# Attention, then top-256 attention, on one core: the first units' scores among the projections, the last five units' fills dealt out anew, the second batch's norm passes one by one

## Chip, core and metric

The kernel runs on one core of a Trainium2 chip. The core has a matrix engine (TensorE, PE in the profile), VectorE (DVE), ScalarE (ACT), GpSimd (POOL) and a queue engine (SyncE, SP) that here only starts transfers. Every engine works through its own instruction list in order and waits on semaphores. The metric is the device time of one execution in microseconds, the lower the better; the figure for a kernel is the median of several runs.

## What is computed

Two layers follow each other on x of 8 x 512 x 32 x 32 (8 batches, 512 channels, 1024 positions), in fp32. Cut to what matters:

```python
# layer 0
h = group_norm(x, 32 groups) * gn_w + gn_b
q, k, v = split(qkv_w @ h + qkv_b)                   # 8 heads of 64
a = softmax(q^T k / 8)                               # 1024 x 1024 per head
x = x + proj_w @ (a v) + proj_b
# layer 1
q, kk, v = wq @ x, wk @ x, wv @ x
idx = top_k(sum over channels of x*x, 256)           # per batch
qs, ks, vs = q, kk, v at idx
a = softmax(clip(LN(qs) LN(ks)^T / sqrt(512), -80, 80))
v at idx = a vs
x = x + wo @ v
```

## The kernel before

**Layer 0** (`layer0`, lines 583 to 1101) is cut into 64 units: 8 batches, 4 pairs of heads, 2 halves of 512 query positions. A unit has 8 steps over key blocks of 128 positions. For each block, PE makes the scores of both heads (`scores`, tile `sc`, a PSUM tile of two banks; two such tiles exist), ScalarE copies them to SBUF (`keep`, tile `e`, 14 buffers) and VectorE keeps a running maximum (`highest`). After the eighth block PE turns the maximum (`turn`, tile `pt`), VectorE reduces and negates it (`negate`, `nm`), PE spreads it back (`spread`, `ns`), VectorE adds it to each kept block (`shift`, "sub"), ScalarE takes the exponential, GpSimd sums the eight blocks (`add`, tile `es`) and PE multiplies them with v (`values`, tile `av`). The sum of all keys goes through PE (`total`, `den`), ScalarE (`take`, `ri`) and VectorE (`invert`, `divide`), giving half of a tile `o`.

The order of all this is written out by hand: `SLOT` (lines 46 to 52) lists the steps of one slot; a plus means that the step is for the next unit, a minus for the one before. All engines but SP follow that order (line 1058). In slot t, then, the scores of unit t + 1 and the exponentials and values of unit t are worked on together.

Between them stand up to five **fills**, `fill0` to `fill4`: blocks of PE work that belong to no softmax. Each is a pair of functions, one for PE and one that empties the PSUM bank. `side(t)` (lines 804 to 827) lists them: projections of q and k (`project`), of v (`v_tokens`), the output projection of the batch before (`project_out`, emptied by VectorE into the residual tile `xr` and then stored), four products `bias_out` in batch 0 that carry v's bias through the output projection, and in the last three units work for layer 1. All fills use one PSUM bank, tile `g` (`ps_g`, one buffer), so a fill waits until the one before it is emptied. Two banks hold `ns` (`ps_m`), one holds `av` (`ps_a`).

Ahead of slot -1 (lines 1069 to 1075) ten fills named `first` run one after the other through that one bank: k and q of the first pair, four parts of v, q of the second pair. Slot -1 then holds unit 0's scores alone.

Group norm of batch b: `norm_stats` reads statistics for one of four channel blocks, `mean_take`, `spread_of`, `variance_take` and `norm_factors` make a factor and a shift, and `norm_apply` rewrites one block of x. For b > 0 these stand in the slots of the batch before, by `NORM` (lines 693 to 699); for b = 1 by `NORM1` in the slots -1 and 0.

**The crossing.** For layer 1, batch 0, `turned_values` and `joint` form wo times wv (tile `wvn`, then `w["vo"]`), `token_rows` transposes x, squares it and stores it, `token_values` makes the values. `begin_layer1` and `finish` (lines 1033 to 1056) hold what is left after unit 63: the last row, all values, the importance of batch 0's tokens and `count_first` (how many tokens lie above each one, on VectorE), and eight output projections of batch 7, each with its own `load_residual` into one of two `xr` buffers. `also` (line 1007) gives each such piece a PSUM bank, two of three from the `sc` tiles, and empties a piece after the next one was filled.

**Layer 1** (`layer1`) follows lists of its own, `BATCH` and `END`, with eight PSUM banks. Its first PE work is `row` of batch 1, tile `b_pt`.

SP starts the loads and stores that these steps name, in an order of its own list; a start that waits holds up those behind it. ScalarE starts the stores of rows (`sx`) and values (`sv`) and the small vectors (`vector_of`, line 146).

## Time and profile before

| what | us |
|---|---|
| median of 3 runs (lowest, highest) | 2684.85 (2680.85, 2687.46) |
| the profiled execution, its time | 2687.3 |
| its span, first to last instruction | 2685.6 |
| PE busy, of the span | 2591.3 (96%) |
| DVE, ACT, POOL busy | 1926.2, 1354.5, 1163.2 |
| mean granted TensorE clock | 0.990 |
| PE busy from 0 to 20, of 20 | 3.5 |
| from 20 to 80, of 60 | 46.86 |
| from 160 to 240, of 80 | 72.50 |
| from 2040 to 2140, of 100 | 82.05 |
| from 2180 to 2200, of 20 | 14.73 |

The profile shows one execution. A line of its timelines has the start, the duration, the engine, the line of the kernel, the operation, the tile written and those read, the shape, how many instructions are merged in it, and in brackets how long the engine was idle before and what ended that idle time. PE's weight loads are a row of their own (PEld). In its table of stretches a group is one engine's busy time with the count of instructions.

### The profile page before, as it was taken

The numbers are of one execution on the slowest core, as the hardware profiler recorded it, in microseconds if no ns is written. First come the engines' busy times: TensorE is split into PE (matmuls) and PEld (weight loads), VectorE is DVE, ScalarE is ACT, GpSimd is POOL, SyncE is SP. The second block draws the span as 40 slices with busy tenths as digits, with TensorE's granted clock in tenths as the row PEclk, the third lists the DMA queues.
The fourth block names the chain that finished last, engine by engine and source line by source line (L and its number), as shares of the span: only waits on it lengthen the run. The fifth ranks groups of instructions, "written<-read, shape, count | busy, mean of one in ns | idle before, by whom it ended". The sixth has DMA issues, their size and how long they took to land.

```text
span 2685.6 us, 27430 instructions
## 1 busy us (share of the span) xinstructions
PE 2591.3 (96%) x9936; PEld 1194.8 (44%) x9936; DVE 1926.2 (72%) x2437; ACT 1354.5 (50%) x1697; POOL 1163.2 (43%) x559
## 2 busy tenths in 40 slices
PE   6999999999999999999999999999998899999995
PEld 3444444444444444444444444444443345555553
DVE  1787878787878688867887787777767636666664
ACT  1555654565556546645665465456555523333331
POOL 0455544455456445445564465445444401211122
PEclk9999999999999999999999999999999999999998
DMA  3000000100100010001000100010002243555555
GB/s 133 1 1 32 1 16 32 48 1 16 62 18 1 24 58 14 1 32 63 0 1 32 63 1 8 24 63 1 16 32 79 75 165 114 197 207 198 194 186 195
DMA packets 79590, 161.21 MB, mean 60 GB/s; under 512 B 12106, under 2 KB 12106, under 8 KB 79456
## 3 DMA queue, kind: packets, MB, share of 16 engines
q1 hardware_dynamic: 52480, 113.27, 11.9%
q10 hardware_dynamic: 19296, 33.58, 3.3%
q0 software_dynamic: 7680, 12.61, 1.6%
q8 instruction: 79, 1.29, 0.2%
q14 instruction: 55, 0.45, 0.1%
HBM read 100.68 MB, written 71.30 MB: 64 GB/s over the span
## 4 chain that ended last, share of the span: by engine, by line
PE 89%; DMA 4%; DVE 3%; ACT 2%; issue 1%; POOL 1%; ACTq 0%; SPq 0%; POOLq 0%; DVEq 0%
PE sc L901 18%; PE av L960 16%; PE g L725 16%; PE g L746 8%; PE g L764 8%; PE b_pv L299 6%; PE b_pp L382 4%; PE den L973 2%; PE ns L938 2%; PE pt L924 2%; DMA sx<-xT 1%; PE last L299 1%; PE b_sc L448 1%; DVE e L944 1%; PE first L725 1%
## 5 line engine op out<-in xcount | busy, mean ns | idle before, releaser
L952 POOL TENSOR_TENSOR es<-es,e 128x1024 f32<-128x1024 f32 x384 | 913.0, 2378 | 327.5 <-ACT e L947 306.7
L909 ACT COPY e<-sc 128x1024 f32<-128x1024 f32 x512 | 508.6, 1013 | 591.5 <-PE sc L901 316.4
L944 DVE TENSOR_TENSOR e<-e,ns 128x1024 f32<-128x1024 f32 x512 | 603.7, 1205 | 2.5 <-PE ns L938 2.2
L947 ACT ACTIVATE e<-e 128x1024 f32<-128x1024 f32 x512 | 531.7, 1056 | 109.5 <-DVE e L944 101.7
L901 PE MATMUL sc<-q,k 64*128 64x512 f32 x2048 | 514.1, 620 | 20.1 <-ACT e L909 17.2
L915 DVE TENSOR_TENSOR high<-sc,high 128x1024 f32<-128x1024 f32 x384 | 469.4, 1222 | 89.2 <-PE sc L901 46.5
L960 PE MATMUL av<-e,v 128*64 128x512 f32 x2048 | 493.6, 603 | 2.7 <-ACT e L947 2.7
L952 POOL TENSOR_TENSOR es<-e,e 128x1024 f32<-128x1024 f32 x64 | 151.4, 2366 | 740.1 <-ACT e L947 740.1
L725 PE MATMUL g<-x,wqkv 128*128 128x512 f32 x976 | 447.6, 601 | 0.0
L901 PEld LDWEIGHTS sc<-q,k 64*128 64x128 f32 x2048 | 177.1, 187 | 349.2 <-issue 178.4
L725 PEld LDWEIGHTS g<-x,wqkv 128*128 128x128 f32 x976 | 176.6, 191 | 224.1 <-issue 224.1
L960 PEld LDWEIGHTS av<-e,v 128*64 128x64 f32 x2048 | 130.0, 136 | 298.6 <-issue 288.5
L985 DVE RECIPROCAL ri<-ri 128x512 f32<-128x512 f32 x64 | 214.6, 3352 | 29.2 <-ACT ri L981 28.8
L746 PE MATMUL g<-wqkv,x 128*128 128x256 f32 x960 | 223.2, 386 | 0.0
L746 PEld LDWEIGHTS g<-wqkv,x 128*128 128x128 f32 x960 | 177.4, 190 | 67.2 <-issue 45.5
L764 PE MATMUL g<-o,wp 128*128 128x512 f32 x448 | 207.2, 605 | 0.0
L299 PE MATMUL b_pv<-w,x 128*128 128x512 f32 x448 | 199.0, 592 | 0.0
L929 DVE TENSOR_REDUCE nm<-pt 128x8 f32<-128x1024 f32 x64 | 78.4, 1224 | 149.5 <-PE pt L924 149.5
L771 DVE SCALAR_TENSOR_TENSOR xr<-g,pb,xr 128x512 f32<-128x512 f32 x56 | 41.9, 749 | 173.1 <-PE g L764 173.1
L764 PEld LDWEIGHTS g<-o,wp 128*128 128x128 f32 x448 | 80.5, 189 | 124.3 <-issue 107.2
L981 ACT COPY ri<-den 128x512 f32<-128x512 f32 x64 | 37.5, 586 | 184.8 <-PE den L973 141.7
L299 PEld LDWEIGHTS b_pv<-w,x 128*128 128x128 f32 x448 | 82.5, 190 | 90.5 <-issue 90.2
(157 smaller groups left out, 2037.5 us busy)
## 6 DMA issues: line engine op xcount, KB each, us to landing
x<-in_x_dram SPq DMA_DIRECT2D x32, 512.0 KB
xr<-in_x_dram SPq DMA_DIRECT2D x64, 256.0 KB
x1d<-xr SPq DMA_DIRECT2D x64, 256.0 KB
x<-x1d SPq DMA_DIRECT2D x32, 512.0 KB
sx<-xT ACTq DMA_DIRECT2D x64, 256.0 KB
sv<-V ACTq DMA_DIRECT2D x64, 256.0 KB
y<-x1d SPq DMA_DIRECT2D x64, 256.0 KB
out_dram<-y SPq DMA_DIRECT2D x64, 256.0 KB
```

The costliest lines, as they stand in the source:

```text
L299: nc.tensor.matmul(pv, x1[b][:, k, ts(j, P)], w["vo"][:, k, :], start=(k == 0), stop=(k == CT - 1),)
L725: nc.tensor.matmul(pq, wqkv[:, k, ts(ot, P)], hs[b][:, k, ts(hf, HALF)], start=(k == 0), stop=(k == CT - 1),)
L746: nc.tensor.matmul(pv[:, ts(j, 2 * P)], hs[b][:, k, ts(2 * part + j, P)], wqkv[:, k, 2 * C + hm * 2 * P : 2 * C + (hm + 1) * 2 * P], start ...
L764: nc.tensor.matmul(po, wp[:, k, ts(mt, P)], os[b * NPAIR + k][:, ts(hf, HALF)], start=(k == 0), stop=(k == CT - 1),)
L901: nc.tensor.matmul(sc[:, hh, :], ks[p][r, ts(j, P)], qs[p][r, ts(hf, HALF)], start=True, stop=True,)
L909: nc.scalar.copy(raw[t, j], banks["s", t, j])
L915: nc.vector.tensor_tensor(high[t], banks["s", t, j], raw[t, 0] if j == 1 else high[t], ALU.max)
L944: nc.vector.tensor_tensor(raw[t, j], raw[t, j], high[t], ALU.add)
L947: nc.scalar.activation(raw[t, j], raw[t, j], AF.Exp, scale=QK_SCALE)
L952: nc.gpsimd.tensor_add(sums[t], raw[t, 0] if j == 1 else sums[t], raw[t, j])
L960: nc.tensor.matmul(avs[t][HD * hh : HD * hh + HD, :], vs[p // 2][:, j, (p % 2) * P + HD * hh : (p % 2) * P + HD * hh + HD], e[:, hh, :], s ...
L985: nc.vector.reciprocal(dens[t], dens[t])
```

## The change

It has five pieces.

1. Ahead of slot -1 only three fills are left: k of the first pair (both halves) and q's first half. They and three more alternate between bank `g` and bank `av`. The three more (q's second half, v's first two parts) are placed in slot -1 after the second, fourth and sixth score block (`FIRST_STEPS`), and their emptying after certain `keep` steps. The other two parts of v and the second pair's q become fills of units 0 and 1, which have five fills each; v_tokens(1, 0) goes from unit 0 to unit 1. The three weight parts are loaded in the order k, q, v, and the vectors `lw` and `lb` are loaded in `constants()`, at slot 2.
2. `bias_out` times four becomes `bias_row` in unit 2 (a row, copied by ScalarE to a buffer of `xr`) and `bias_columns` in unit 3 (four transposes and one add on VectorE).
3. For batch 1 the four statistics stand in slot -1, two after the maximum of block 3 and two after that of block 7, and the four `norm_apply` of slot 3 stand after `div`, after `sub` of block 5, after `sub` of block 6 and after the maximum of block 7.
4. Units 60 to 63: unit 60 has six fills, with project(31, 1, 1) put off to unit 61 and three `turned_values` taken in; unit 61 has the last `turned_values` and three `joint`, unit 62 the last `joint`, three `token_values` and a row, unit 63 two `token_values`, two rows beside the fills, and three output projections of batch 7.
5. `also` empties each piece directly after the next fill, and takes bank `g` at listed counts. `begin_layer1` holds five rows and two values, `finish` five output projections, one value and the counts. The residuals of batch 7 are loaded into free `e` buffers (`spare`), but for two in `xr`.

```diff
-            for part in range(3):
+            for part in (1, 0, 2):
                 nc.sync.dma_start(wqkv[:, :, ts(part, C)], wsrc[:, :, ts(part, C)])
...
             NORM1 = {
-                (-1, "max", 7): [(norm_stats, 0), (norm_stats, 1)],
-                (0, "div", 0): [(norm_stats, 2)], (0, "sub", 5): [(norm_stats, 3)],
+                (-1, "max", 3): [(norm_stats, 0), (norm_stats, 1)],
+                (-1, "max", 7): [(norm_stats, 2), (norm_stats, 3)],
+                (3, "div", 0): [(norm_apply, 0)], (3, "sub", 5): [(norm_apply, 1)],
+                (3, "sub", 6): [(norm_apply, 2)], (3, "max", 7): [(norm_apply, 3)],
             }
...
-                        if b == 1 and at <= 0 and name != "neg":
+                        if b == 1 and name != "neg" and at != 2:
                             todo = NORM1.get((at, name, j), [])
...
-            def bias_out(mt):
+            def bias_row():
                 def fill(pt):
                     for k in range(CT):
                         nc.tensor.matmul(
-                            pt[:, :1], wp[:, k, ts(mt, P)],
-                            bqkv[:, 2 * CT + k : 2 * CT + k + 1],
-                            start=(k == 0), stop=(k == CT - 1),
+                            pt, bqkv[:, 2 * CT + k : 2 * CT + k + 1].broadcast_to([P, P]),
+                            wp[:, k, :], start=(k == 0), stop=(k == CT - 1),
                         )
                 def empty(pt):
-                    nc.vector.tensor_add(pb[:, mt : mt + 1], pt[:, :1], bp[:, mt : mt + 1])
+                    resid["row"] = rp.tile([P, C], F32, tag="xr", name="bias_row")
+                    nc.scalar.copy(resid["row"], pt)
+                return fill, empty
+
+            def bias_columns():
+                def fill(pt):
+                    row_ = resid.pop("row")
+                    for mt in range(CT):
+                        nc.tensor.transpose(pt[:, ts(mt, P)], row_[:, ts(mt, P)], ident)
+                def empty(pt):
+                    nc.vector.tensor_add(pb, pt.rearrange("p (m q) -> p m q", q=P)[:, :, 0], bp)
                 return fill, empty
...
+                if t == 0:
+                    todo = [v_tokens(0, 2), v_tokens(0, 3)] + todo + [project(1, 0, 0)]
+                    return todo
+                if t == 1:
+                    todo += [project(1, 0, 1), v_tokens(1, 0)]
...
-                if 1 <= at <= CT:
-                    if b:
-                        todo += [project_out(b - 1, at - 1, h) for h in range(NH)]
-                    else:
-                        todo.append(bias_out(at - 1))
+                if b and 1 <= at <= CT:
+                    todo += [project_out(b - 1, at - 1, h) for h in range(NH)]
+                if 2 <= t <= 3:
+                    todo.append((bias_row, bias_columns)[t - 2]())
+                if t == UNITS - 4:
+                    held.append(todo.pop(1))
+                    todo = [
+                        todo[0], todo[1], turned_values(0), todo[2], turned_values(1),
+                        turned_values(2),
+                    ]
                 if t == UNITS - 3:
-                    todo += [turned_values(mt) for mt in range(CT)] + [joint(0)]
+                    todo += [held.pop(), turned_values(3)] + [joint(c) for c in range(3)]
                 if t == UNITS - 2:
-                    todo += [joint(c) for c in range(1, CT)] + [token_rows(j) for j in range(2)]
+                    todo += [joint(3)] + [token_values(j) for j in range(3)] + [token_rows(0)]
                 if t == UNITS - 1:
-                    todo += [token_rows(j) for j in range(2, 7)]
+                    todo += [token_values(3), token_values(4)]
+                    todo += [project_out(B - 1, mt, 0) for mt in range(3)]
...
             def also(step):
-                if len(last) % 3 == 2:
+                if count_of[0] in (4, 7, 10, 13, 16):
...
                 step[0](pt)
+                flush()
                 last.append((step[1], pt))
-                if len(last) > 1:
-                    last[-2][0](last[-2][1])
+                count_of[0] += 1
+
+            def flush():
+                while last:
+                    end, pt = last.pop()
+                    end(pt)
...
+            outs = [(CT - 1, 0)] + [(mt, 1) for mt in range(CT)]
             def begin_layer1():
-                also(token_rows(7))
-                also(token_values(0))
+                for one in outs[:2]:
+                    load_residual(B - 1, *one)
+                for one in (
+                    token_rows(3), token_rows(4), token_values(5), token_rows(5), token_rows(6),
+                    token_rows(7), token_values(6),
+                ):
+                    also(one)
                 finite(0, 0)
-                also(token_values(1))
                 tiles["imp", 0] = spare("imp_0")
                 also(importance(0))
                 also(importance(1))
-                also(token_values(2))
-                count_first(0)
-                count_first(1)
+                flush()
+                for j in range(2):
+                    count_first(j)
                 total(UNITS - 1, 0)
             def finish():
-                outs = [(mt, hf) for hf in range(NH) for mt in range(CT)]
                 for i, one in enumerate(outs):
-                    load_residual(B - 1, *one)
+                    if i > 1:
+                        load_residual(B - 1, *one, spare(f"xr_last_{3 + i}")[:, :HALF])
                     also(project_out(B - 1, *one))
-                    if i < 5:
-                        also(token_values(3 + i))
-                    if i < 6:
-                        count_first(2 + i)
-                last[-1][0](last[-1][1])
+                    count_first(2 + i)
+                    if i == 0:
+                        also(token_values(7))
+                count_first(7)
+                flush()
...
-                first = [project(0, which, hf) for which in (1, 0) for hf in range(NH)]
-                first += [v_tokens(0, part) for part in range(2 * NH)]
-                first += [project(1, 0, hf) for hf in range(NH)]
-                for i, (begin, end) in enumerate(first):
-                    pt = ps_g.tile([P, HALF], F32, tag="g", name=f"first_{i}")
-                    begin(pt)
-                    end(pt)
+                FIRST_STEPS = {
+                    ("sc", 1): project(0, 0, 1), ("sc", 3): v_tokens(0, 0), ("sc", 5): v_tokens(0, 1),
+                    ("keep", 0): "empty", ("keep", 3): "empty", ("keep", 4): "empty",
+                }
+                pending = []
+                def first(step):
+                    if step == "empty":
+                        end, pt = pending.pop(0)
+                        end(pt)
+                    else:
+                        pool, tag = ((ps_g, "g"), (ps_a, "av"))[len(firsts) % 2]
+                        firsts.append(step)
+                        pt = pool.tile([P, HALF], F32, tag=tag, name=f"first_{len(firsts)}")
+                        step[0](pt)
+                        pending.append((step[1], pt))
+                firsts = []
+                for step in (
+                    project(0, 1, 0), project(0, 0, 0), "empty", project(0, 1, 1), "empty", "empty",
+                ):
+                    first(step)
...
+                    if t == UNITS - 1:
+                        for mt in range(3):
+                            load_residual(B - 1, mt, 0, spare(f"xr_last_{mt}")[:, :HALF])
                     for name, ahead, j in order:
                         if 0 <= t + ahead < UNITS and (name, t) != ("den", UNITS - 1):
                             STEPS[name](t + ahead, j)
+                        if t == -1 and (name, j) in FIRST_STEPS:
+                            first(FIRST_STEPS[name, j])
                         norms(t, name, j)
+                        if t == UNITS - 4 and name == "empty" and j == 4:
+                            fill(t, 5)
+                        if t == UNITS - 4 and (name, j) == ("exp", 6):
+                            empty(t, 5)
+                        if t == UNITS - 1 and (name, j) == ("fill", 1):
+                            also(token_rows(1))
+                            also(token_rows(2))
```

More of the change, by code (lines that the diff above doesn't have):

```diff
@@ L174, in attention_then_topk_attention @@
     a_dram = [dram.tile([TOP, C], F32, tag=f"sa{b}", name=f"sa{b}") for b in range(B)]
-    lw = vector_of(ln_w, CT, "lw")
-    lb = vector_of(ln_b, CT, "lb")
     before = const.tile([P, P], F32, tag="before", name="before")
@@ L183, in constants @@
     def constants():
+        w["ln_w"] = vector_of(ln_w, CT, "lw")
+        w["ln_b"] = vector_of(ln_b, CT, "lb")
         make_lower_triangular(nc, before, val=1.0, diag=False)
@@ L434, in scale @@
                     t[:, c, :], pt[:, a, :], AF.Identity,
-                    bias=lb[:, c : c + 1], scale=lw[:, c : c + 1],
+                    bias=w["ln_b"][:, c : c + 1], scale=w["ln_w"][:, c : c + 1],
                 )
@@ L438, in scale @@
                 nc.vector.tensor_scalar(
-                    t[:, c, :], pt[:, a, :], lw[:, c : c + 1], lb[:, c : c + 1],
+                    t[:, c, :], pt[:, a, :], w["ln_w"][:, c : c + 1], w["ln_b"][:, c : c + 1],
                     ALU.mult, ALU.add,
@@ L776, in project_out, with load_residual @@
                 return fill, empty
-            def load_residual(b, mt, hf):
-                xr = rp.tile([P, HALF], F32, tag="xr", name=f"xr_{b}_{mt}_{hf}")
+            def load_residual(b, mt, hf, xr=None):
+                if xr is None:
+                    xr = rp.tile([P, HALF], F32, tag="xr", name=f"xr_{b}_{mt}_{hf}")
                 nc.sync.dma_start(xr, x[b, ts(mt, P), ts(hf, HALF)])
@@ L815, in side @@
                     todo.append(v_tokens(m + 1, part))
-                if 1 <= at <= CT:
-                    if b:
-                        todo += [project_out(b - 1, at - 1, h) for h in range(NH)]
-                    else:
-                        todo.append(bias_out(at - 1))
+                if b and 1 <= at <= CT:
[8 more added lines that the diff above has]
+                    ]
                 if t == UNITS - 3:
-                    todo += [turned_values(mt) for mt in range(CT)] + [joint(0)]
+                    todo += [held.pop(), turned_values(3)] + [joint(c) for c in range(3)]
                 if t == UNITS - 2:
-                    todo += [joint(c) for c in range(1, CT)] + [token_rows(j) for j in range(2)]
+                    todo += [joint(3)] + [token_values(j) for j in range(3)] + [token_rows(0)]
                 if t == UNITS - 1:
-                    todo += [token_rows(j) for j in range(2, 7)]
+                    todo += [token_values(3), token_values(4)]
+                    todo += [project_out(B - 1, mt, 0) for mt in range(3)]
                 return todo
+            held = []
             def turned_values(mt):
@@ L1003, in layer0 @@
             FIRST, LAST = by_age[0][2], by_age[-1][2]
-            last = []
+            last, count_of = [], [0]
             def also(step):
-                if len(last) % 3 == 2:
-                    pt = ps_g.tile([P, HALF], F32, tag="g", name=f"last_{len(last)}")
+                if count_of[0] in (4, 7, 10, 13, 16):
+                    pt = ps_g.tile([P, HALF], F32, tag="g", name=f"last_{count_of[0]}")
                 else:
-                    pt = ps_s.tile([P, 2, HALF], F32, tag="s", name=f"last_{len(last)}")[:, 0, :]
+                    pt = ps_s.tile([P, 2, HALF], F32, tag="s", name=f"last_{count_of[0]}")[:, 0, :]
                 step[0](pt)
+                flush()
                 last.append((step[1], pt))
-                if len(last) > 1:
-                    last[-2][0](last[-2][1])
+                count_of[0] += 1
[3 more added lines that the diff above has]
+                    end(pt)
             def importance(j):
```

## The prediction

> **What bounds the kernel now.** I read the page's busy times and chain of waits first, then the timeline of the TensorE (PE) queue where its busy share drops, then the other engines' timelines at those places.
>
> Chain of waits of the page (shares of the span):
>
> ```profile
> PE 89%; DMA 4%; DVE 3%; ACT 2%; issue 1%; POOL 1%; ACTq 0%; SPq 0%; POOLq 0%; DVEq 0%
> ```
>
> PE sets the end. Busy time by stretch (span, then busy us of PE, PEld, DVE, ACT, POOL, then granted clock):
>
> ```profile
> 240.00:280.00 40.00, 40.00 (x162) 17.71 (x160) 32.19 (x27) 24.42 (x28) 19.23 (x9) 1.00 0.00 0
> ```
>
> From 240 to 2040 PE never waits: a unit is the sum of its PE instructions. In the timeline, a unit with three fills repeats every 28.6 us (distance of two `pt` blocks), with five every 35.9. A gain must come from stretches where PE waits or runs at half clock. There are three. First, the beginning (start, busy us, then in brackets the wait before it):
>
> ```profile
> 55.14 3.70 PE L725 MATMUL first<-x,wqkv 128*128 128x512 f32 x8 [0.68 <-ACT v L755]
> 59.62 3.70 PE L725 MATMUL first<-x,wqkv 128*128 128x512 f32 x8 [0.78 <-ACT q L733]
> 63.25 1.99 PE L901 MATMUL sc<-q,k 64*128 64x512 f32 x8
> 67.27 2.39 PE L901 MATMUL sc<-q,k 64*128 64x512 f32 x8 [2.03 <-ACT e L909]
> 72.03 2.96 PE L901 MATMUL sc<-q,k 64*128 64x512 f32 x8 [2.37 <-ACT e L909]
> 77.01 3.78 PE L901 MATMUL sc<-q,k 64*128 64x512 f32 x8 [2.02 <-ACT e L909]
> 80.72 4.88 PE L725 MATMUL g<-x,wqkv 128*128 128x512 f32 x8
> ```
>
> Ten fills share one PSUM bank, so each waits for the previous copy; then unit 0's scores run alone and wait for ScalarE and VectorE, with nothing else on PE; the waits bring half clock (3.78 and 4.88 where 1.99 and 3.70 is usual). Second, the second batch's norm in unit 3, on VectorE, GpSimd and PE:
>
> ```profile
> 191.59 8.30 DVE L686 TENSOR_SCALAR x<-x,gsc,gsh 128x1024 f32<-128x1024 f32 x4
> 188.28 10.34 POOL L952 TENSOR_TENSOR es<-es,e 128x1024 f32<-128x1024 f32 x4 [1.72 <-ACT e L947]
> 203.38 3.79 PE L901 MATMUL sc<-q,k 64*128 64x512 f32 x8 [4.45 <-ACT e L909]
> ```
>
> Four passes stand together on VectorE for 8.30 us and everything behind them is late. Third, the end of layer 0, PE then VectorE:
>
> ```profile
> 2119.11 0.66 PE L238 MATMUL g<-ident,x 128*128 128x128 f32 x4 [3.42 <-ACT xT L246]
> 2130.22 1.11 PE L960 MATMUL av<-e,v 128*64 128x512 f32 x4 [2.71 <-ACT e L947]
> 2196.73 2.82 PE L238 MATMUL b_pt<-ident,x 128*128 128x128 f32 x12 [5.27 <-DVE xr L771]
> 2195.92 0.75 DVE L771 SCALAR_TENSOR_TENSOR xr<-last,pb,xr 128x512 f32<-128x512 f32 x1 [7.11 <-DMA xr<-in_x_dram]
> ```
>
> Units 60 to 63 have small transposes (0.6 us) as fills where others have 3.6 us products, so PE waits for the softmax; then the output projections run back to back, and the last residual load is late.
>
> **What the Trainium skill says.** "SBUF — State Buffer", Who interferes with whom: VectorE and GpSimd share a port pair; a tensor_scalar in its two-port mode and a GpSimd instruction exclude each other for a whole instruction. The trace agrees: a norm pass takes 0.80 us at the least, but a median of 2.02 over all 32, one per GpSimd add in unit 3. "TensorE: Matmul & The Clock Gate", What's actually happening: the clock halves after an idle window of about 3.4 us. Here it halved already after three waits of some 2 us each, so I count half clock wherever such waits cluster, and none after a single wait below 2 us (at 2045 the waits of 1.34 and 0.91 brought none).
>
> **Part 1, the beginning.** A fill costs 3.63 us between two others, a pair of scores 1.92, a kept copy 1.01, a maximum 1.23, a bank's copy 0.59 to 0.69. Laid out from the unchanged first matmul at 17.65 (it waits for the norm; the weights' new order changes nothing there, k having landed as second part already): k0, q0, k1 alternate over two banks without a wait to 30.3. First two scores to 32.3, q1 to 35.9, next two to 37.8, v0 to 41.4. By then ScalarE has kept the third score pair (39.1 to 40.1, after its maximum) but VectorE has two norm_stats inserted (2 x 1.48 us, 39.1 to 42.1) ahead of the next maximum, 43.35: a wait of 1.0. Scores to 44.3, v1 to 48.0, scores to 49.95, v2 to 53.6, transposes to 54.6; the other two statistics end at 54.5, just in time; the negated maximum ends 55.9, sc1 56.85, `ns` begins about 57, against 88.86: 32 us earlier. But seven fills are done there instead of eleven; four come later, 4 x 3.63 = 14.5. Net **17.5**, which is the 6.6 us of bank waits, 6.7 of score waits and 4.3 of half clock, all but 1. If the first score also waits for k1's copy, 0.8 less.
>
> The removed loads of lw and lb free 2 x 0.45 us of ScalarE's queue under the wait for x: nothing. In unit 2 they cost the same 0.9, where ScalarE idles 3.0 us before `ri`: nothing, else 0.9.
>
> **Part 2, units 0 to 4.** PE's excess there is 0.28 + 0.89 + 0.89 + 1.27 + 4.45 + 0.89 of waits and (3.79 - 1.99) + (4.84 - 3.70) of half clock: 11.6. The three 0.89 before `sc6` in units 1, 2 and 4 (in unit 3 it is inside the 4.45) arise because bias_out's add holds VectorE until PE has made the bias, with only 2.7 us of PE work after it. Afterwards units 0 and 1 have five fills, unit 2 a full bias_row (its copy is on ScalarE), unit 4 none: these waits go. Unit 2 keeps 1.27 (norm_factors before `nm`). Unit 3 keeps bias_columns with its add: about 1.0, having less PE work than before. The norm passes, each behind a GpSimd add at up to 2.07: after div, 1.6, hidden (the maximum that it delays ended at 190.5, the score behind it went at 193.2); after sub5, under the 4.3 us that VectorE waits for the bias; after sub6 and max7, 2 x 2.07 under fill 0 (3.6) and the transposes: about 1.1 shows at `pt`. New excess 3.4, bounds 1.3 to 8. bias_row plus columns cost 3.63 + 0.53 for four times 0.98: 0.2 more. Net **8.0**.
>
> **Part 3, units 60 on.** Excess before: unit 60 1.48; unit 61 1.34, 0.91, 1.24, 1.63; unit 62 0.2, 0.28; unit 63 1.80, 1.98, half clock 2.6, 3.42, 1.02, 2.71, half clock 1.5; the crossing 5.27 and half clock after it (28 transposes until 2203) 2.8: together 30.2. After the change PE's work is the same; what is exposed:
> - Unit 60: a small transpose before `sc4` leaves 2.8 us less cover, some 1.2; the pair of transposes sharing the bank and then `sc6`, 1.5.
> - Unit 61: fill 1 still small, 1.24. Products cover the rest.
> - Unit 62: four products and one row. The row's copies on ScalarE (1.4, and its store) delay exp2 and exp6, so the sums on GpSimd: 1.2 at `den`.
> - Unit 63: fill 2 (a projection) shares the bank with token_values(4), whose copy stands behind token_rows(1) (0.60 + 0.19 + 0.58 + 0.33) and two exponentials (2.1): free about 12.4 us after `pt`, wanted at 9.4: 3.0.
> - begin_layer1: five rows cost ScalarE 1.7 each; PE waits about 1. Counts 0 and 1 (3.8) stand before the reciprocal (3.35), which still ends as token_values(7) does.
> - finish: five projections instead of eight; VectorE ends two counts (3.8) and its add about 1.9 after PE. A single wait: no half clock.
>
> Sum 11 to 13, against 30.2: **17**. The SP queue: three residual loads go out before the projections, into exp buffers; the last three stand behind stores and x1 of batch 2, the very last issued some 7 us before it is wanted (4.06 us in the trace). Cover gone costs 2 to 4.
>
> Layer 1 keeps its order and PE is busy 100.00 of 100 us from 2200, then 98, so the shift is carried to the end.
>
> **Sum.** 17.5 + 8.0 + 17 = 42.5. The profiled span is 2685.6 (its run 2687.3); the span becomes 2643. The runs' median is 2684.85, so I forecast 2684.85 - 42.5 = about 2643. Differences below 0.3% (8 us) are about what a measurement of this kernel can tell from no change.
>
> **Rivals.**
> - *The end does not pay* (0.15). Another 12 to 17 us of waits: one bank for all of unit 63's projections, and ScalarE with rows, values and exponentials. For it: ScalarE ends waits there already (3.42, 2.71). Against: it is 50% busy or so. Gain 25.5 and up to 5: 2654 to 2659.
> - *VectorE becomes the bound at the beginning* (0.10). It has about 24 us per unit of 29; statistics and passes at 2.8 (the longest in the trace) would overfill unit 3 (24 + 11 against 29.2, 6 us) and cost about as much ahead of unit 0. Parts 1 and 2 then give 14 instead of 25.5: 2654. Against: the passes may fall between GpSimd's adds at 0.80.
> - *More than forecast* (0.06). Half or all of my 16 us of new waits (1.0 + 3.4 + 12) do not occur: 2627 to 2635.
> - *Slower* (0.04). x1 of batch 0 is loaded on SP only when project(31, 1, 1) has released batch 7's x; that now runs at the end of unit 60, no longer as its second fill. token_values(0) needs it as second fill of unit 62. Issue about 2047, 2 MB at the 249 GB/s seen at 2020 is 8.4 us, so 2058; wanted near 2087. PE waits for every us beyond 29 of delay, and the kernel is slower from 71 us of delay on. A delay of 100 gives 2713. Nothing on SP before it is that late in this trace.
> - *No difference* (0.03): a delay of about 71 by the same wait.
>
> **How the numbers follow.** Forecast 0.62, around 2643. Its own range, from the bounds above (part 2 from 3 to 10, part 3 from 10 to 22), is 2635 to 2654. To hold 8 in 10 the range is 2631 to 2660, taking in most of the first two rivals. Faster is 0.62 + 0.15 + 0.10 + 0.06 = 0.93, the same 0.03, slower 0.04.
>
> **What the profile after would show.** Scores of unit 0 between full fills, `ns` of unit 0 near 57 and no half clock from 22 to 100; no 4.45 in unit 3 and norm passes in four places; a wait near 3 us in unit 63 ahead of the first projection by the bank's copy; row transposes of batch 1 beginning 42 us earlier, less than 2.5 us after the last projection, at full clock. Wrong if `ns` is later than 65, if units 60 to 63 hold over 16 us of PE waits, or if layer 1 is longer than before.

## The result and the profile after

The changed kernel takes 2645.02 us, the median of four runs (2641.74 to 2646.70), against 2685.41 (2680.85 to 2687.46) for the kernel before in the same rounds. The ratio is 0.985, with a 95% interval of 0.9833 to 0.9867: 36 to 45 us less, 40.4 by the medians. The profiled execution took 2641.74, its span is 2640.0, against 2687.3 and 2685.6. The two profiled executions thus lie near opposite ends of their kernels' ranges: their spans differ by 45.6, five more than the medians, and the traces of this section are this pair.

PE still sets the end. Chain of waits on the page of the changed kernel:

```profile
PE 90%; DMA 3%; DVE 3%; ACT 1%; issue 1%; POOL 1%; ACTq 0%; SPq 0%; POOLq 0%; DVEq 0%
```

PE's busy time fell from 2591.3 to 2578.1, though the products are the same but for the bias: 13 us of the 45.6 is, for the most part, work done at full clock that ran at half clock before. The other 32 are waits. The stretch that the prediction took as its rule, 240 to 280, is as before: PE busy 40.00 of 40.

**The beginning.** Timeline of PE, changed kernel:

```profile
16.45 13.54 PE L727 MATMUL first<-x,wqkv 128*128 128x512 f32 x24 [3.88 <-DVE x L686]
29.92 1.99 PE L930 MATMUL sc<-q,k 64*128 64x512 f32 x8
31.84 3.70 PE L727 MATMUL first<-x,wqkv 128*128 128x512 f32 x8
...
42.70 1.13 PE L930 MATMUL sc<-q,k 64*128 64x512 f32 x4 [0.53 <-DVE high L944]
...
55.24 1.13 PE L930 MATMUL sc<-q,k 64*128 64x512 f32 x4 [0.26 <-DVE nm L958]
56.30 1.09 PE L967 MATMUL ns<-ident,nm 128*128 128x128 f32 x8
```

Three fills run without a wait, then scores stand between fills at their usual 1.99. `ns` begins 32.6 us earlier than before (88.86). The table of stretches for 22 to 100, which has PE's busy time third and the granted clock third from the end, says the same of the changed kernel:

```profile
22.00:100.00 78.00, 77.09 (x291) 38.47 (x291) 44.95 (x48) 37.94 (x44) 18.91 (x8) 1.00 0.04 15
```

and of the kernel before:

```profile
22.00:100.00 78.00, 64.60 (x210) 32.47 (x210) 22.44 (x25) 24.45 (x29) 5.26 (x3) 0.93 0.08 29
```

**Units 2 and 3.** The 4.45 us wait and its half clock are gone. Three short waits are left on PE:

```profile
159.08 1.99 PE L930 MATMUL sc<-q,k 64*128 64x512 f32 x8 [1.11 <-DVE nm L958]
180.95 1.99 PE L930 MATMUL sc<-q,k 64*128 64x512 f32 x8 [0.89 <-ACT e L938]
187.50 1.07 PE L953 MATMUL pt<-ident,high 128*128 128x128 f32 x8 [0.94 <-DVE high L944]
```

VectorE's timeline has the four passes in four places, 5.70 us in all where they took 8.30 together:

```profile
167.27 1.35 DVE L686 TENSOR_SCALAR x<-x,gsc,gsh 128x1024 f32<-128x1024 f32 x1
174.39 0.81 DVE L686 TENSOR_SCALAR x<-x,gsc,gsh 128x1024 f32<-128x1024 f32 x1
182.17 2.73 DVE L686 TENSOR_SCALAR x<-x,gsc,gsh 128x1024 f32<-128x1024 f32 x1
187.28 0.81 DVE L686 TENSOR_SCALAR x<-x,gsc,gsh 128x1024 f32<-128x1024 f32 x1
```

**Units 60 to 63 and the crossing**, PE, every wait over 0.5 us:

```profile
2003.37 1.99 PE L930 MATMUL sc<-q,k 64*128 64x512 f32 x8 [0.80 <-ACT e L938]
2013.69 0.66 PE L862 MATMUL g<-ident,pair 128*128 128x128 f32 x4 [1.38 <-ACT wvn L869]
2029.31 1.13 PE L930 MATMUL sc<-q,k 64*128 64x512 f32 x4 [1.23 <-DVE high L944]
2089.38 1.08 PE L1002 MATMUL den<-es,ones 128*64 128x512 f32 x4 [1.22 <-POOL es L981]
2100.33 5.40 PE L766 MATMUL g<-o,wp 128*128 128x512 f32 x8 [2.69 <-ACT V L313]
2126.16 3.70 PE L299 MATMUL last<-w,x 128*128 128x512 f32 x8 [0.91 <-ACT xT L246]
2155.17 1.53 PE L238 MATMUL b_pt<-ident,x 128*128 128x128 f32 x12 [1.77 <-DVE xr_last L773]
```

Unit 63's first projection waits 2.69 us for ScalarE to copy token_values(4) out of the shared bank, and then takes 5.40 instead of 3.70: half clock. Batch 1's transposes start 41.6 us earlier (2196.73 before) and at full clock.

Where the gain lies, by start times of the same instruction in the two traces:

| up to | before | after | shift |
|---|---|---|---|
| first product | 17.65 | 16.45 | 1.20 |
| `ns` of unit 0 | 88.86 | 56.30 | 32.56 (four fills still owed) |
| `pt` of unit 5 | 242.32 | 216.19 | 26.13 |
| `ns` of unit 60 | 2017.95 | 1991.81 | 26.14 |
| first `b_pv` of layer 1 | 2203.05 | 2159.89 | 43.16 |
| end of span | 2685.6 | 2640.0 | 45.6 |

Between units 5 and 60 nothing moved by more than 0.01 us.

### The profile page after: what moved, and what is told of

Same layout as the page of the kernel before. It is cut to its first block, busy times and chain, and to the rows that moved or that the text cites. A ratio compares the mean times of both kernels' runs of the same rounds, so it can differ in the third digit from the quotient of the medians.

```text
span 2640.0 us, 27385 instructions
## 1 busy us (share of the span) xinstructions
PE 2578.1 (98%) x9916; PEld 1185.7 (45%) x9916; DVE 1922.1 (73%) x2434; ACT 1352.7 (51%) x1698; POOL 1163.8 (44%) x559
## 4 chain that ended last, share of the span: by engine, by line
PE 90%; DMA 3%; DVE 3%; ACT 1%; issue 1%; POOL 1%; ACTq 0%; SPq 0%; POOLq 0%; DVEq 0%
PE sc L930 18%; PE av L989 17%; PE g L727 16%; PE g L748 8%; PE g L766 8%; PE b_pv L299 5%; PE b_pp L382 4%; PE ns L967 2%; PE den L1002 2%; PE pt L953 2%; DMA sx<-xT 1%; PE b_sc L448 1%; PE first L727 1%; PE b_po L527 1%; DMA y<-x1d 1%
## 5 line engine op out<-in xcount | busy, mean ns | idle before, releaser
L727 PE MATMUL g<-x,wqkv 128*128 128x512 f32 x992 | 453.0, 599 | 0.0
L748 PE MATMUL g<-wqkv,x 128*128 128x256 f32 x992 | 230.5, 385 | 0.0
L766 PE MATMUL g<-o,wp 128*128 128x512 f32 x472 | 219.9, 609 | 2.7 <-ACT V L313 2.7
L748 PEld LDWEIGHTS g<-wqkv,x 128*128 128x128 f32 x992 | 183.4, 190 | 68.0 <-issue 44.7
L958 DVE TENSOR_REDUCE nm<-pt 128x8 f32<-128x1024 f32 x64 | 78.4, 1225 | 146.7 <-PE pt L953 146.4
```

What stands on the lines that cost most here:

```text
L727: nc.tensor.matmul(pq, wqkv[:, k, ts(ot, P)], hs[b][:, k, ts(hf, HALF)], start=(k == 0), stop=(k == CT - 1),)
L748: nc.tensor.matmul(pv[:, ts(j, 2 * P)], hs[b][:, k, ts(2 * part + j, P)], wqkv[:, k, 2 * C + hm * 2 * P : 2 * C + (hm + 1) * 2 * P], start ...
L766: nc.tensor.matmul(po, wp[:, k, ts(mt, P)], os[b * NPAIR + k][:, ts(hf, HALF)], start=(k == 0), stop=(k == CT - 1),)
```

## The experiments

Spans and start times are those of each run's profiled execution. The runs stand in four series, in which the kernel before had medians of 2685.41, 2684.18, 2685.64 and 2684.04; the changed kernel had 2645.02 in the first and 2642.96 in the third. So two or three us between medians of different series mean nothing by themselves, and the sizes are read from the traces. "pt5" is the start of `pt` of unit 5, where the beginning and the norm are over.

### The beginning undone

The ten first fills and the fills of units 0 and 1 as before the change; all else of the change stays.

```diff
...
-                FIRST_STEPS = { ... }
...
-                for step in (project(0, 1, 0), project(0, 0, 0), "empty", ...):
-                    first(step)
+                first = [project(0, which, hf) for which in (1, 0) for hf in range(NH)]
+                first += [v_tokens(0, part) for part in range(2 * NH)]
+                first += [project(1, 0, hf) for hf in range(NH)]
+                for i, (begin, end) in enumerate(first):
+                    pt = ps_g.tile([P, HALF], F32, tag="g", name=f"first_{i}")
+                    begin(pt)
+                    end(pt)
...
```

> The changed kernel with the old beginning (ten fills ahead of slot -1 through one bank, units 0 and 1 with their old fills; all else as changed). Theory of the prediction: the beginning is worth 17.5 us, so ns of unit 0 begins 32 us later than in the changed kernel (near 88) with eleven fills done instead of seven, the bank waits (0.78 and 0.68) and half clock in unit 0's scores are back, and the time is about 2662. Rival (VectorE or ScalarE limit units 0 and 1 once they carry five fills, so the beginning gained little): less than 10 us more than the changed kernel, below 2655.

Measured: 2660.88 (2659.70 to 2662.82), ratio 0.9912 (0.9895 to 0.9928); pt5 at 234.69, 18.5 later than in the changed kernel. The waits and the half clock are back (PE):

```profile
66.75 2.39 PE L924 MATMUL sc<-q,k 64*128 64x512 f32 x8 [2.03 <-ACT e L932]
71.50 1.13 PE L924 MATMUL sc<-q,k 64*128 64x512 f32 x4 [2.37 <-ACT e L932]
74.38 2.08 PE L924 MATMUL sc<-q,k 64*128 64x512 f32 x4 [1.74 <-DVE high L938]
78.48 3.78 PE L924 MATMUL sc<-q,k 64*128 64x512 f32 x8 [2.03 <-ACT e L932]
```

The beginning is worth 18.5 us in the trace and 15.9 by the medians; nothing later gives it back. The wait of 1.74 is not of the old kernel: it comes from two norm_stats, which in this run stand among scores that nothing covers. From the first product to `ns` this run takes 73.10 and the kernel before 71.21, so some 1.9 of the 18.5 is not the old beginning's.

### The banks alone

As above, but the ten fills take banks `g` and `av` in turn, each emptied after the next was issued. The scores stay behind them. This splits the 18.5. The diff is against the run above.

```diff
+                pending = []
                 for i, (begin, end) in enumerate(first):
-                    pt = ps_g.tile([P, HALF], F32, tag="g", name=f"first_{i}")
+                    pool, tag = ((ps_g, "g"), (ps_a, "av"))[i % 2]
+                    pt = pool.tile([P, HALF], F32, tag=tag, name=f"first_{i}")
                     begin(pt)
-                    end(pt)
+                    for done, bank in pending:
+                        done(bank)
+                    pending = [(end, pt)]
+                pending[0][0](pending[0][1])
```

> The changed kernel with the ten fills ahead of unit 0's scores as before the change, but taking their banks from two pools in turn, each copied out after the next fill was issued; the scores stay behind the fills. It splits the 17.5 us of the beginning. Theory, by my prediction's own terms: the 6.6 us of bank waits go, the 8.2 us of score waits (2.03, 2.37, 1.74, 2.03 in the kernel with the beginning undone) and the half clock behind them (1.9 for the scores, 0.5 for the fill) stay, since they come from ScalarE and VectorE at work on scores with nothing else on TensorE: ns of unit 0 at 83.0 instead of 89.64, and a time of about 2654. Rival: the nine short waits of 0.7 were part of what halved the clock; without them the half clock goes too, and ns begins near 80.5, time about 2652. Second rival: most of the gain was in the banks and the scores' waits shrink with them, since the copies no longer stand in ScalarE's queue ahead of the kept scores; ns below 79 and time below 2650.

Measured: 2652.02 (2649.66 to 2656.84), ratio 0.9877 (0.9861 to 0.9894); `ns` of unit 0 at 81.22 instead of 89.64, pt5 at 226.28. PE:

```profile
32.28 13.98 PE L748 MATMUL first<-wqkv,x 128*128 128x256 f32 x64
46.09 7.03 PE L727 MATMUL first<-x,wqkv 128*128 128x512 f32 x16
53.05 1.99 PE L924 MATMUL sc<-q,k 64*128 64x512 f32 x8
57.06 3.34 PE L924 MATMUL sc<-q,k 64*128 64x512 f32 x8 [2.03 <-ACT e L932]
62.77 2.08 PE L924 MATMUL sc<-q,k 64*128 64x512 f32 x4 [2.37 <-ACT e L932]
...
69.75 3.79 PE L924 MATMUL sc<-q,k 64*128 64x512 f32 x8 [2.03 <-ACT e L932]
```

`ns` is at neither 83.0 nor 80.5, and the time cannot tell the theory's 2654 from the first rival's 2652. The trace can: without the bank waits the clock is halved just the same, even more (3.34 where 2.39 stood), so that rival's mechanism falls. The second rival's `ns` below 79 falls by the number. The theory was too low by what a bank wait costs. Four fills in a row take 13.98, 3.50 each; alone in their bank they followed each other every 4.40 (37.04 to 41.44 in the run above). A wait that the trace prints as 0.68 thus costs 0.9, the end of a product no longer overlapping the start of the next. From first product to first score the ten fills took 46.2 before this edit and 36.6 with it. Of these 9.6, about 0.8 is the first fill at a clock not yet full, and 8.8 stand where I had 6.6; the scores, more of them at half clock, give 1.3 back. By pt5, two banks are worth 8.4 of the 18.5, and putting the scores between the fills the other 10.1.

### The end undone

Units 60 to 63, `begin_layer1`, `finish`, `also` and the residual loads as before the change.

```diff
...
                 if t == UNITS - 3:
-                    todo += [held.pop(), turned_values(3)] + [joint(c) for c in range(3)]
+                    todo += [turned_values(mt) for mt in range(CT)] + [joint(0)]
                 if t == UNITS - 1:
-                    todo += [token_values(3), token_values(4)]
-                    todo += [project_out(B - 1, mt, 0) for mt in range(3)]
+                    todo += [token_rows(j) for j in range(2, 7)]
...
+                outs = [(mt, hf) for hf in range(NH) for mt in range(CT)]
                 for i, one in enumerate(outs):
-                    if i > 1:
-                        load_residual(B - 1, *one, spare(f"xr_last_{3 + i}")[:, :HALF])
+                    load_residual(B - 1, *one)
...
```

> The changed kernel with the old units 60 to 63, begin_layer1, finish and residual loads. Theory: 17 us more than the changed kernel, about 2662, the 5.27 wait before the first row of batch 1 and the half clock after it are back, and the shift at unit 60 is the full 26 us. Rival (layer 1 starts when its loads and gathers allow, whatever the end of layer 0 does): under 8 us more, and layer 1 shorter than in the changed kernel.

Measured: 2660.10 (2655.89 to 2662.21), ratio 0.9903 (0.9886 to 0.9919). PE's crossing line, then VectorE's line that it waits for:

```profile
2171.78 2.82 PE L238 MATMUL b_pt<-ident,x 128*128 128x128 f32 x12 [4.85 <-DVE xr L773]
```

```profile
2170.97 0.75 DVE L773 SCALAR_TENSOR_TENSOR xr<-last,pb,xr 128x512 f32<-128x512 f32 x1 [6.69 <-DMA xr<-in_x_dram]
```

The late residual load and the half clock behind it are back. From pt5 to the first `b_pv` it takes 1962.9, against 1943.7 with the change (and 1960.7 in the kernel before): 17 to 19 in the traces, 15.1 by the medians. Of the 2 us between 1962.9 and 1960.7, 1.6 are half clock in unit 61 behind waits of 1.34 and 0.93; the kernel before had waits of 1.34 and 0.91 there and full clock. Layer 1 from `b_pv` on took 482.7, not less, so a kernel that is late there does not catch up, and the rival falls.

### The four norm passes together again

```diff
-                (3, "div", 0): [(norm_apply, 0)], (3, "sub", 5): [(norm_apply, 1)],
-                (3, "sub", 6): [(norm_apply, 2)], (3, "max", 7): [(norm_apply, 3)],
+                (3, "sub", 5): [(norm_apply, c) for c in range(CT)],
```

> The changed kernel with the four norm passes of batch 1 together after sub of block 5, as before. Theory: in unit 3 they take about 8.3 us again, one per GpSimd add, the score behind them waits 4 to 4.5 us with half clock after it (some 2.9), the waits of 0.89 and 0.94 go: 5 to 6 us more than the changed kernel, about 2650.5. Rival (it was the bias product that made unit 3 late, and with bias_columns four passes fit): within 1.5 us of the changed kernel.

Measured: 2647.87 (2646.43 to 2649.78), ratio 0.9863 (0.9846 to 0.9879), 2.9 more by the medians; pt5 at 221.33, 5.14 more. The passes on VectorE, and the scores on PE behind them:

```profile
173.12 8.32 DVE L686 TENSOR_SCALAR x<-x,gsc,gsh 128x1024 f32<-128x1024 f32 x4
```

```profile
184.93 3.79 PE L929 MATMUL sc<-q,k 64*128 64x512 f32 x8 [4.87 <-ACT e L937]
```

The trace confirms the 5 to 6 where it was expected; by the first `b_pv` 3.3 are left, mostly because unit 63's first projection ran at full clock in this run (3.70 instead of 5.40). The time alone does not confirm it: 2.9 is not clear of the differences between series.

### Four bias products instead of row and columns

The products stand in units 2 to 5.

```diff
...
-                if 2 <= t <= 3:
-                    todo.append((bias_row, bias_columns)[t - 2]())
+                if 2 <= t <= CT + 1:
+                    todo.append(bias_out(t - 2))
```

> The changed kernel with the four bias_out products back, in units 2 to 5 (one later than before, since unit 1 has five fills now). Theory: each of these units waits 0.89 ahead of its seventh score block, 3.6 in all against 0.89 now, the work is 0.2 less: about 2.5 us more, shown by the waits of the trace rather than by the time. Rival (the waits came from the norm work beside them): no such waits in unit 4 and 5.

Measured: 2649.54 (2644.37 to 2650.19), ratio 0.9862 (0.9846 to 0.9879); 2.7 us lost by `pt` of unit 6, counted from `ns` of unit 0. The rest of the trace's difference lies in layer 1, which took 486.3 from `b_pv` on (480.1 in the changed kernel) and which the edit does not touch; why is open. Each unit with such a product has its wait (PE):

```profile
147.46 1.99 PE L919 MATMUL sc<-q,k 64*128 64x512 f32 x8 [0.89 <-ACT e L927]
179.34 1.99 PE L919 MATMUL sc<-q,k 64*128 64x512 f32 x8 [0.89 <-ACT e L927]
211.07 1.99 PE L919 MATMUL sc<-q,k 64*128 64x512 f32 x8 [0.89 <-ACT e L927]
241.61 1.99 PE L919 MATMUL sc<-q,k 64*128 64x512 f32 x8 [0.89 <-ACT e L927]
```

ScalarE is named, but it had waited for VectorE, whose add stood 2.56 to 4.50 us for PE's bias product with everything else queued behind it.

### The small vectors first again

`lw` and `lb` loaded ahead of everything, as before the change.

```diff
+    lw = vector_of(ln_w, CT, "lw")
+    lb = vector_of(ln_b, CT, "lb")
...
     def constants():
-        w["ln_w"] = vector_of(ln_w, CT, "lw")
-        w["ln_b"] = vector_of(ln_b, CT, "lb")
...
```

> The changed kernel with the two small vectors lw and lb loaded first again. Theory (formed from the two traces: the third load of x waits on SP for a transfer that these two started, 5.13 us for the four issues against 1.81): four issues take about 5 us again and the first projection starts near 17.6 instead of 16.45. The prediction had it at nothing. Rival (x landed earlier by chance): first projection stays within 0.3 of 16.45.

Measured, one execution: first product at 17.46; the other runs with the late vectors have it at 16.25 to 16.65. SP's longest wait in the first 12 us of this run:

```profile
SPq L603 <- DMA lw<-in_ln_w_dram: 3.0, 1, 3.0
```

and in the kernel before:

```profile
SPq L602 <- DMA lw<-in_ln_w_dram: 3.5, 1, 3.5
```

The queue that starts the loads of x stands until the small vector that ScalarE's queue started has landed, so x and the whole norm come later. In the changed kernel there is no such wait ahead of x's loads; the first is 2.2 us, behind `gw`, ahead of the weights. The 1.0 us did not reach the end here: `ns` of unit 0 began at 56.40 (56.30 in the changed kernel) and the time was 2643.23. The first 24 products begin at half clock and took between 12.34 and 13.58 in the runs, and this spread is as large: full clock is first recorded at 21.64 here, 4.2 us after the first product, and at 22.47, 6.0 us after it, in the changed kernel's trace. Half of that difference is 0.9 us.

### The passes right behind the negated maximum

All four after `nm` of unit 3.

```diff
-                (3, "div", 0): [(norm_apply, 0)], (3, "sub", 5): [(norm_apply, 1)],
-                (3, "sub", 6): [(norm_apply, 2)], (3, "max", 7): [(norm_apply, 3)],
...
+                        if b == 1 and (at, name) == (2, "neg"):
+                            todo = [(norm_apply, c) for c in range(CT)]
```

> The changed kernel with batch 1's four norm passes all right behind the negated maximum of unit 3, where GpSimd is idle. Theory (a pass costs 2 us or more only behind a GpSimd add): about 0.8 us each, 3.1 together, as at the very start; the reciprocal and the first sub are 3 us late. Rival (a pass costs 2 us wherever ScalarE and PE are busy): 8 us together.

Measured, one execution: 2643.99; pt5 at 216.09 against 216.19. The passes on VectorE, and what waits for them on PE:

```profile
158.68 2.97 DVE L686 TENSOR_SCALAR x<-x,gsc,gsh 128x1024 f32<-128x1024 f32 x4
```

```profile
168.40 1.13 PE L930 MATMUL sc<-q,k 64*128 64x512 f32 x4 [1.07 <-DVE high L944]
```

Where GpSimd has no adds, a pass takes 0.74; 2.97 for all four, against 5.70 spread out and 8.30 among the adds. It gains nothing: the wait of 1.07 stands in place of the 0.94 at `pt`, since VectorE is behind at both places.

### A bank for unit 63, and the factors moved

```diff
-                (3, "div", 0): [(norm_apply, 0)], (3, "sub", 5): [(norm_apply, 1)],
-                (3, "sub", 6): [(norm_apply, 2)], (3, "max", 7): [(norm_apply, 3)],
+                (3, "div", 0): [(norm_apply, 0)], (3, "sub", 5): [(norm_apply, 1), (norm_apply, 2)],
+                (3, "max", 7): [(norm_apply, 3)],
+                (2, "sub", 5): [(norm_factors,)],
...
+                    if (t, i) == (UNITS - 1, 2):
+                        banks[t, i] = ps_s.tile([P, 2, HALF], F32, tag="s", name=f"g_{t}_{i}")[:, 0, :]
...
```

> The changed kernel with three more moves: unit 63's third fill (the first output projection of batch 7) gets one of the two score tiles in place of bank g, batch 1's norm_factors go from the maximum of block 7 of unit 2 to its sub of block 5, and the third norm pass of unit 3 joins the second after sub of block 5. Theory: the wait of 2.69 in unit 63 and the half clock after it (1.7), the 1.11 before sc1 of unit 3 and the 0.94 before pt go: 6.4 us less than the changed kernel, about 2638.5. Rival for unit 63 (the softmax chain of unit 63 sets its end, not the bank): the wait moves to the next values and the crossing comes less than 1.5 us earlier.

The changed kernel itself ran beside it:

> The changed kernel itself, for comparison in the same series: about 2645.

Measured: 2639.29 (2638.16 to 2641.97), ratio 0.9829 (0.9815 to 0.9842), and 2642.96 (2639.69 to 2645.67), ratio 0.9841 (0.9827 to 0.9854) for the changed kernel: 3.7 less by the medians where 6.4 was expected, and the intervals overlap. Unit 63's wait is gone with its half clock:

```profile
2095.98 3.70 PE L767 MATMUL g<-o,wp 128*128 128x512 f32 x8
```

`b_pt` comes 4.5 us earlier than in the changed kernel's first trace, counted from `ns` of unit 0. The norm's edits gave nothing; PE's waits only moved:

```profile
149.86 1.99 PE L934 MATMUL sc<-q,k 64*128 64x512 f32 x8 [1.60 <-ACT e L942]
180.55 1.99 PE L934 MATMUL sc<-q,k 64*128 64x512 f32 x8 [1.43 <-ACT e L942]
```

That is 3.03 where 1.11 + 0.89 + 0.94 = 2.94 stood. The factors take VectorE about 8 us there (138.5 to 146.4), two of their small steps 2.19 each, and the maximum behind them is late.

### That bank, with the passes early

> The changed kernel with two edits already seen apart: unit 63's third fill in a score tile, and the four norm passes of the second batch right after the negated maximum of unit 3. Theory: the first gains the 2.69 of the wait and the 1.7 of half clock behind it, the second nothing (its wait of 1.07 stands in place of 0.94): 4.4 less than the changed kernel, about 2639, the same as the kernel with that bank and with the factors moved. Rival: without the half clock being due in every execution the gain is 2.7 on the mean, and the time is about 2641.

Both edits were shown above. Measured: 2639.58 (2636.86 to 2644.44), ratio 0.9829 (0.9815 to 0.9843). `b_pt` at 2150.66 is 4.4 us before that of the early passes alone (2155.03), as expected. But the crossing ran at half clock this time (`b_pt` to `b_pv` 6.41 where it was 4.72), so 1.7 of it was given back. The two versions are equal (2639.29 and 2639.58), and 3 to 6 us below the changed kernel's two medians, with intervals that overlap; that the bank takes unit 63's wait away is shown by both traces.

## Why the prediction was right, point by point

The forecast was 42.5 us less; the span became 45.6 less and the median 40.4. Each step against its measurement in the two traces, which together show five us more than the medians do:

| step | forecast | measured |
|---|---|---|
| beginning: `ns` of unit 0 earlier, less four fills | 32 - 14.5 = 17.5 | 32.56 - 14.5 = 18.1 |
| its waits left | 1.0 | 0.53 + 0.26 |
| units 0 to 4 | 8.0 | 26.13 - 18.06 = 8.1 |
| their waits left | 1.27, 1.0, 1.1 | 1.11, 0.89, 0.94 |
| unit 60 on, to `b_pv` | 17 | 43.16 - 26.14 = 17.0 |
| units 60, 61, 62 | 1.2 + 1.5, 1.24, 1.2 | 0.80 + 1.38, 1.23, 1.22 |
| unit 63's bank | 3.0 | 2.69, and 1.7 of half clock |
| `begin_layer1`, crossing | 1, 1.9 | 0.91, 1.77 |
| layer 1 | 0 | 2.4 |

**Right, and shown.** The waits were worked out by laying each engine's queue beside PE's, and each came within 0.5 us, that half clock apart. Undoing the beginning, the end, the bias and the norm passes each brings its loss back near its expected size in the traces, and the parts are separate: pt5 stays within 1.4 us when the end is undone (214.86), and from pt5 to `b_pv` it takes 1941.9 with the beginning undone, 1943.7 without, the difference being unit 63's half clock. ScalarE does end unit 63's wait as it was said: row copies, two exponentials of 2.00 together, then the copy of V, which ends at 2100.28:

```profile
2097.81 2.00 ACT L976 ACTIVATE e<-e 128x1024 f32<-128x1024 f32 x2 [0.40 <-DVE e L973]
2099.72 0.56 ACT L313 COPY V<-g 128x512 f32<-128x512 f32 x1
```

**Step that failed: "the removed loads of lw and lb ... nothing", with the first product "unchanged".** It was 1.2 earlier. The prediction looked at ScalarE's queue, which starts these loads, and not at SP's, which stood behind their landing. It should have read the waits of SP at the start. From the first product to `ns` it then took 39.85 for a forecast of 39.35. So 1.2 of the 18.1 came from outside the forecast's terms; without it the beginning gives 16.9 for 17.5.

**Step mis-sized: the bank waits as 6.6 us.** The sum of the printed waits left out the overlap that products lose; with the banks alone they came to 8.8. The net of the beginning still came out, because it was laid out forward from the durations and not summed from the waits. The forecast's check of it did not hold in itself: 6.6 + 6.7 + 4.3 less 1 is 16.6 and not the 17.5 of the layout.

**Step mis-sized: unit 63's 3.0 us.** The wait was 2.69, but half clock followed, 1.7 us that no step had. The prediction's rule counted half clock where waits cluster and none after a single one below 2 us; a single one near 3 it priced as if the rule reached that far.

What decides it can be read from the traces. In all twelve, the record of the granted clock changes only on a grid of 3.41 us, and this grid lies differently to the first instruction in each. In the changed kernel nearly the whole wait fell into one interval of the grid, and the next interval ran at half clock (start and end, length, PE busy, granted clock):

```profile
2097.77:2101.18 3.41, 0.85 (x2) 1.00 0.21 81
2101.18:2104.60 3.42, 3.42 (x5) 0.50 0.19 72
```

With the beginning undone the grid cut the same wait in two, and the clock stayed full:

```profile
2114.15:2117.56 3.41, 1.99 (x13) 1.00 0.20 77
2117.56:2120.97 3.41, 2.14 (x5) 1.00 0.20 77
2120.97:2124.39 3.42, 3.42 (x14) 1.00 0.04 17
```

From the first full clock up to 2180 us the twelve traces have 7561 intervals at full clock. In 20 of them PE was busy for a share of 0.449 or less, and each was followed by one at half clock. In the others the share was 0.453 or more, and none was. (Near the end of layer 1 it is less sharp: one interval with a share of 0.51 was followed by half clock, and one with 0.45 was not.) So it takes some 1.9 us of waits within one interval, in one piece or in several. By these lengths a single wait of 2.69 ends at half clock for about two in three positions of the grid (an estimate); it did in five runs of eight.

The sum hid the 1.7. The listed terms of Part 3 come to 11.0, and the 17 was taken from the upper end of "11 to 13". Measured are 10.0 of these waits, 1.7 of half clock and 1.1 at the crossing, 12.8. At the crossing the single wait of 1.77 brought no half clock here, as said; yet from `b_pt` to `b_pv` only 1.6 us was gained (6.32 to 4.72) where 2.8 was counted, since the small `b_pn` products between them took 1.71 instead of 0.61, beside VectorE's picks, which they read.

The Trainium skill ("TensorE: Matmul & The Clock Gate", What's actually happening) asks for an idle window of about 3.4 us, and says that the window is free-running. The grid agrees in its length and in lying differently in each run. That the window must be idle throughout is not what the traces show: a wait of 2.69 was enough where it lay in one window, and so was a window with PE busy for a share of 0.449.

**The port.** The Trainium skill ("SBUF — State Buffer", Who interferes with whom) has the shared pair held for a whole instruction. Passes at 0.74 with no add beside them and at 2.08 among adds agree. The forecast allowed up to 2.07 for each of the last three passes; they took 0.81, 2.73 and 0.81.

**Rivals.** "The end does not pay" and "VectorE becomes the bound" are out by the table: the end gave 17, and the waits for VectorE that are left in the first units are 0.26 to 1.11 each. "Slower" turned on batch 0's x1: SP starts its four loads at 2019.92 (forecast 2047 less the 26 of the shift). The transfers end before 2034, as the stretch behind it in the changed kernel moved nothing (last column, GB/s):

```profile
2030.00:2034.00 4.00, 4.00 (x12) 1.44 (x9) 4.00 (x5) 3.33 (x4) 3.92 (x2) 1.00 0.73 269
2034.00:2038.00 4.00, 4.00 (x19) 1.46 (x20) 3.87 (x5) 2.80 (x4) 3.63 (x3) 1.00 0.00 0
```

token_values(0) starts at 2059.99 without a wait: 26 us of slack, where 29 was said (its 2058 has 2.6 us more than 2047 and 8.4, without a term for them). A kernel with that load delayed was not tried.

**Layer 1.** Its 2.4 us are not the change's: from `b_pv` to the end it took 480.1 in this execution, 481.3 in the changed kernel's other trace, 482.5 in the kernel before and 481.6 to 486.3 in the experiments. That they came on top of the forecast in this pair is chance.

## What to carry over

Forecast a reordered stretch by laying out each engine's queue beside the bounding engine with measured durations; this gave every new wait to within 0.5 us, where adding up the printed waits came out 2 us short for ten fills. It does not give the half clock behind a wait: that comes where some 1.9 us of waits fall into one interval of a grid that moves from run to run, so a wait of 2 to 3 us has it by chance, and several shorter ones close together can too. Read the waits of the queue that starts the first loads before calling a small load free: it can hold a queue that never names it. Work put on an engine that is behind only moves its wait, as three placings of the same norm passes and factors show (2.9 to 3.1 us of waits each time). A bank for the fill that waits takes the wait away.

## What was not expected of the hardware

- **Where a wait lies on a fixed grid decides on half clock.** The 2.69 us wait of unit 63 stands in eight of the runs. The projection behind it took 5.28 to 5.40 in five, where an interval of the grid was left with PE busy for a share of 0.21 to 0.33, and 3.70 in three (beginning undone, norm passes together, banks alone), where none went below 0.45. In the kernel before, even the wait of 3.42 in unit 63 brought none: the grid left shares of 0.48 and 0.52.
- At the crossing, waits of 1.54 to 2.20 us brought some half clock in three runs (banks alone, and both with the new bank; `b_pt` to `b_pv` 5.04, 5.18 and 6.41), with shares of 0.36, 0.42 and 0.44, and none in seven (4.72 to 4.73), with 0.48 to 0.57. In the run with the end undone, waits of 1.34 and 0.93 fell into one interval together (0.38) and brought it.
- Half clock that depends on the run may be part of the spread of the times: the changed kernel's first four executions had a mean granted clock of 0.996 at 2641.74 and of 0.993 to 0.994 at 2643.42 to 2646.70. Only the first was traced, so this is not shown.
- **A queue waits for another queue's load.** SP stood 3.0 to 3.5 us behind a small vector that ScalarE's queue had started and that nothing in x's loads needs. What ties the two together, the program's own waits or the hardware, the traces do not show.
